# Raw keys per batch, node masks loaded once, and stores that alternate with fetches on the GpSimd queue of a two-layer graph kernel

## The chip, the core and the metric

The kernel runs on one NeuronCore of one Trainium2 chip. The core has five instruction queues: TensorE (PE), VectorE (DVE), ScalarE (ACT), GpSimd (POOL) and SyncE (SP, which only issues DMAs). The metric is the device time of one execution in microseconds (us). A change of under about 1% (19 us) can't be told from no change here: three runs of this same kernel lie between 1901.12 and 1918.54 us.

## The reference, cut to what matters

Sixteen graphs ("batches") of 1024 nodes with 64 channels go through two layers. In the first, every node receives the adjacency-weighted mean of its neighbours. In the second, each node drops some of its neighbours ("dilation"), takes three quantiles of each channel over the neighbours that are left, and runs a small two-layer perceptron on the result.

```
# layer 0
h = max(layernorm(x), 0)
x = x + (adj / clip(sum(adj, 2), 1)) @ h
# layer 1
h = max(layernorm(x), 0)
adj_ = where(eye, 1, adj);  nb = (adj_ > 0) & ~eye;  m = nb.sum(-1)
rank = cumsum(nb, -1) - 1
skip = where(m > 10, (m + 1) // 2, 1);  do_dil = (skip > 1) & mask
removed = nb & do_dil & ((rank + 1) % skip == 0)
valid = where(removed | removed.T, 0, adj_) > 0
agg = sum over tau of weight * (quantile tau of h over the valid neighbours)
y = (relu((h + agg) @ W1 + b1) @ W2 + b2) * mask
x = x + y
```

`adj` is 16 x 1024 x 1024 in float32 (64 MB). Most of it is zero: a node has a list of neighbours, short for most nodes and long for a few. `nodemask` is 16 x 1024 bytes.

## The kernel before, in words

**Lists instead of matrices.** The kernel turns each row of `adj` into a list of neighbour numbers, sorts all nodes of a group of four batches by the length of their lists, and then works on 128 nodes at a time whose lists have nearly the same length. It runs in two parts that overlap:

- *Per batch* (loops over 16 batches, each with eight blocks of 128 rows). `loads` (line 570) fetches `xt` (the nodes), `mrow` (the mask, 8 x 128 bytes) and eight tiles `at` of `adj`, all on SP. `beginnings` (588) normalises the nodes on ACT and DVE, and turns the mask on PE so that nodes lie on partitions. `signs` (610) takes signs on ACT; `listing` (627) multiplies them with a descending key (`keyed`) and takes the eight largest keys of each quarter row, 32 in all, into `rec`. `transposes` and `products` (667 on) do layer 0 on PE. `channels` (733) normalises again, into `row`. `endings` (747) writes the 32 keys of each node into `row` beside its channels, works out the node's place in the sorted order, and scatters the eight blocks of `row` to `srt` in DRAM with eight indirect DMAs on POOL.
- *Per group* of four batches. `group` (1196) reads the sorted keys back as `recs`, merges them to at most 16 per node (`keys`), and makes indices of them (`idx`). Then it adds one `Job` (841) for each list length. A job fetches neighbours' rows with one indirect DMA on POOL for every 128 neighbours (`places<-tab`), removes the dropped ones, sorts on DVE with a network of min and max, weighs, sums on PE, runs the perceptron, and stores 128 finished rows with one indirect DMA on POOL (`out_dram<-y`). Four lists of the longest nodes go through `long_lists` (1333) at the end (`lplaces<-whole`).

**What sets the order.** The order of DVE and POOL is written out by a planner (`Plan`, line 236) while the program is built, and the other queues are ordered from it. Streams of work yield the engine that they need next, the time from which they are ready, and a rank; `run` always takes the stream with the smallest pair (time at which it can begin, rank), so the rank decides only among streams that can begin at once. In this order each engine then works strictly in sequence. `endings` asks for POOL with a rank of `rank - 3000`, ahead of everything. Fetches of short jobs have the rank 100 times their group's number, plus a small number; stores of finished rows take the rank -1000 while fewer than 16 fetches of begun jobs are still to be issued, and 5000 otherwise (`urgent`). `scatter` (828) puts a one-column memset (`turn`) between two scatters to the same tensor that would follow each other directly. A buffer `places` is one of four, so that a fetch may have to wait until an earlier job is done with its buffer.

**What the change and the prediction touch.**

- Keys. `keyed` counts down over a whole row from a start that depends on the block of 128 rows, so `rec` holds N + 128 t - j for neighbour j of a node in block t. In `endings` eight ACT instructions, one per block, subtract 128 t and clip at zero while they copy to `row` (`bias=before[:, t:t + 1]`, lines 757 to 760).
- Masks. Sixteen small DMAs (576), casts (593), PE transposes (604) and ACT copies (606, 607: mask and node number into the last two columns of `row`).
- Stores. The rank function `first` (749) of the scatter of `row`, and the POOL request of `layers` (1190) for finished rows.

Of the kernel before, what the change touches and what calls it, by code (L numbers as in the profile page):

```python
# [9 lines left out]
F32 = mybir.dt.float32  # L10
# [233 lines left out]
class Plan:  # L244
# [25 lines left out]
    def room(self, name, bufs):  # L270

        tiles = self.slots.get(name, ())
        if len(tiles) < bufs:
            return 0.0
        old = tiles[-bufs]
        return INF if self.users[old] else max(self.used.get(old, 0.0), self.ready.get(old, 0.0))

    def at(self, *tiles):
        return max(self.ready.get(t.tensor.name, INF) for t in tiles)
# [104 lines left out]
def list_path(ctx, tc, x, adj, nodemask, w1, b1, w2, b2, out, go):  # L384
# [93 lines left out]
    wt0 = consts.tile([P, 1], F32, name="wt0")  # L478
    nc.vector.memset(wt0, QUANTILES[0][1])

    before = consts.tile([P, NT], F32, name="before")
    nc.vector.tensor_scalar(before, col_f[:, :NT], -float(P), None, op0=OP.mult)

    idle = consts.tile([P, 1], F32, name="idle")
    turn = consts.tile([P, 1], F32, name="turn")
# [80 lines left out]
    def known(st, *names):  # L566

        return max(at(st[name]) if name in st else INF for name in names)

    def loads(pool, now):  # L570
        def nodes(st, b):
            yield "SP", lambda: room("xt", 3)
            st["xt"] = new(pool, [P, NT, C], F32, "xt", 3, users=1)
            nc.sync.dma_start(st["xt"], x[b].rearrange("(t p) c -> p t c", p=P))
            st["mrow"] = new(tiny, [NT, P], U8, "mrow", 3)
            nc.sync.dma_start(st["mrow"], nodemask[b].rearrange("(t p) -> t p", p=P))

        yield from nodes(batch[0], 0)
        for b, st in enumerate(batch):
            now[0] = b  # L580
            for t in range(NT):
                if t == 2 and b + 1 < B:
                    yield from nodes(batch[b + 1], b + 1)
                yield "SP", lambda: room("at", 5)
                st["rows"][t] = new(pool, [P, N], F32, "at", 5, users=2)
                nc.sync.dma_start(st["rows"][t], adj[b, t * P:(t + 1) * P, :])

    def beginnings(pool, now):

        for b, st in enumerate(batch):  # L590
            now[0] = b
            yield "DVE", lambda: max(known(st, "xt", "mrow"), room("h0", 3), room("row", 4))
            mrow_f = new(tiny, [NT, P], F32, "mrow_f", 2)
            nc.vector.tensor_copy(mrow_f, st["mrow"])

            h0 = new(pool, [P, NT, C + 1], F32, "h0", 3, users=2)
            nc.vector.memset(h0[:, :, C:], 1.0)
            row = st["row"] = new(pool, [P, NT, RW], F32, "row", 4, users=1)
            nc.vector.memset(row[:, :, C:W], -1.0)
            yield from normed(h0[:, :, :C], st["xt"])  # L600
            st["h0"] = h0
            yield "PE", lambda: max(at(mrow_f), room("ps_small", 3))
            pm = new(ps_s, [P, HALF], F32, "ps_small", 3, users=1)
            nc.tensor.transpose(pm[:, :NT], mrow_f, ident[:NT, :NT])
            yield "ACT", lambda: at(pm)
            nc.scalar.copy(row[:, :, RW - 1], pm[:, :NT])
            nc.scalar.copy(row[:, :, RW - 2], row_f)
            free(pm)

    def signs(pool, now):  # L610
        for b, st in enumerate(batch):
# [134 lines left out]

    def endings(pool, now):

        first = lambda rank: rank - 3000
        for b, st in enumerate(batch):  # L750
            now[0] = b
            g = max(g for g in range(NG) if FIRST[g] <= b)
            size = GROUPS[g]
            yield "ACT", lambda: known(st, "rec", "row") if st["listed"] == NT else INF
            rec, total, row = st["rec"], st["total"], st["row"]

            for t in range(NT):
                nc.scalar.activation(
                    row[:, t, R0:R0 + 8 * NSEG], rec[:, t, :], AF.Relu, bias=before[:, t:t + 1]
                )  # L760


            yield "DVE", always
            found = new(pool, [P, NT, 8 * NSEG], BF, "found", 1)
            nc.vector.tensor_scalar(found, rec, 0.0, None, op0=OP.is_gt)
            d = new(tiny, [P, NT], F32, "d", 2)
            nc.vector.tensor_reduce(d, found, AX.X, OP.add)
            full = new(tiny, [P, NT], F32, "full", 2)
            nc.vector.tensor_reduce(
                full, found.rearrange("p t (s e) -> p t s e", e=8)[:, :, :, 7], AX.X, OP.max  # L770
            )
            nc.vector.scalar_tensor_tensor(d, full, float(STEPS[0]), d, op0=OP.mult, op1=OP.max)
            nc.vector.tensor_scalar(d, d, float(STEPS[0]), None, op0=OP.min)
            for s in STEPS[1:]:
                nc.vector.scalar_tensor_tensor(d, total, float(s), d, op0=OP.is_gt, op1=OP.add)
            free(rec)
            free(total)
            hot = new(tiny, [P, CLS, NT], BF, "hot", 2)
            nc.vector.tensor_tensor(
                hot, cls, d.unsqueeze(1).to_broadcast([P, CLS, NT]), OP.is_equal  # L780
            )
            yield "PE", lambda: max(at(hot), room("ps_small", 3))
            pc = new(ps_s, [P, HALF], F32, "ps_small", 3, users=1)
            K = CLS * NT
            flat = hot.rearrange("p c t -> p (c t)")
            nc.tensor.matmul(pc[:, :K], earlier, flat, start=True, stop=True)
            nc.tensor.matmul(pc[:, K:2 * K], ones, flat, start=True, stop=True)
            yield "DVE", lambda: at(pc) + SLACK
            base = new(tiny, [P, K], F32, "base", 2)
            nc.vector.tensor_tensor_scan(  # L790
                base, pc[:, K:2 * K], zeros[:, :K], 0.0, op0=OP.add, op1=OP.add
            )
            nc.vector.tensor_tensor(base, base, pc[:, K:2 * K], OP.subtract)
            nc.vector.tensor_tensor(base, base, pc[:, :K], OP.add)
            free(pc)
            nc.vector.tensor_tensor(base, base, flat, OP.mult)
            pos = new(tiny, [P, NT], F32, "pos", 2)
            nc.vector.tensor_reduce(pos, base.rearrange("p (c t) -> p t c", t=NT), AX.X, OP.add)
            low = new(tiny, [P, NT], I32, "low", 2)
            nc.vector.tensor_copy(low, pos)  # L800
            nc.vector.tensor_scalar(low, low, LSUB - 1, None, op0=OP.bitwise_and)
            if size == 2:
                aside = new(tiny, [P, 2, NT], F32, "aside", 2)
                for e, by in enumerate((-32.0, 64.0)):
                    nc.vector.tensor_scalar(
                        aside[:, e, :], pos, 64.0 / (e + 1), by, op0=OP.is_lt, op1=OP.mult
                    )
                for e in range(2):
                    nc.vector.tensor_tensor(pos, pos, aside[:, e, :], OP.add)
            nc.vector.tensor_scalar(  # L810
                pos, pos, float(size), float(LSUB * (b - FIRST[g])), op0=OP.mult, op1=OP.add
            )
            to = new(pool, [P, NT], I32, "to", 2)
            nc.vector.scalar_tensor_tensor(to, low, float(1 - size), pos, op0=OP.mult, op1=OP.add)
            for t in range(NT):
                yield "POOL", lambda: max(at(to), at(row)) + LOOSE if "normed" in st else INF, first
                scatter(srt[g], row[:, t, :], to[:, t:t + 1], sorts[g])
            free(row)
            progress["batches"] = b + 1
# [21 lines left out]
    class Job:  # L841
# [291 lines left out]
        def layers(self, terms, sources):  # L1133
# [53 lines left out]
                free(py)  # L1187

            for t in range(T):
                yield "POOL", lambda: at(y) + LATE  # L1190
                top = HP if self.half and t == 0 else P
                scatter(out_rows, y[:top, t, :], self.nodes_i[:top, t:t + 1], scatters)
            free(y)
# [2 lines left out]
    def group(g, kept=grp, name=""):  # L1196
# [53 lines left out]
        keys = new(kept, [P, NTAU, 16], F32, name + "keys", 1 if name else 2)  # L1250
        nc.vector.memset(keys, 0.0)
        left = tiny.tile([P, 8 * NSEG], F32, name="left")
        for t in range(begin, NTAU):
            nc.vector.max(out=keys[:, t, :8], in_=lists[:, t, :])
            if caps[t] > 8:
                nc.vector.match_replace(
                    out=left, in_to_replace=keys[:, t, :8], in_values=lists[:, t, :],
                    imm_value=0.0,
                )
                nc.vector.max(out=keys[:, t, 8:], in_=left)  # L1260
            if t % 8 == 0:
                yield "DVE", always

        assert all(cap <= T_THRESH for cap in caps[begin + 1:])
        fst = slice(begin, begin + 1)
        skip = dilation(m[:, fst], mask[:, fst], 1)
# [462 lines left out]
```

## Time and profile before

| | |
|---|---|
| median of three runs | 1902.93 us (1901.12, 1902.93, 1918.54) |
| the profiled execution, whole | 1904.97 us |
| its span, first to last instruction | 1902.9 us, 16005 instructions |
| indirect DMAs on POOL | 931: 128 of `srt<-row`, 496 of `places<-tab`, 163 of `lplaces<-whole`, 128 of `out_dram`, 8 of `tab<-drop`, 8 of `gat_rows` |
| start of the eight scatters of a batch | 68, 101, 140, 176 us for the first four, then 243, 284, 376, 492, 585, 642, 738, 826, 949, 981, 1098, 1139 us |
| start of the last group's fetch of `gat_rows` | 1161 us |
| memsets `turn` | 215, 25.7 us busy |

All times below come from that one execution, which is 2.04 us longer than the median. A row of the profile names engine, operation, the tile written and the tiles read, the number of instructions, their summed and mean time, and the time in which the engine stood idle ahead of them together with what ended it. "issue" there means that the engine waited for nothing that the profile shows, "remote" that the releaser is not known. Since nearly all instructions are recorded under the one line of the planner's wrapper (L238), groups are told apart by their tiles.

### The profile page before, as it was taken

How to read it: one execution, taken by the hardware profiler on the slowest of the kernel's cores; microseconds unless marked ns; L12 is line 12 of the kernel's file. 1: busy time of each engine (PE TensorE's matmuls, PEld its weight loads, DVE VectorE, ACT ScalarE, POOL GpSimd, SP SyncE). 2: the span in 40 equal slices, each digit the busy share in tenths (PEclk: the TensorE clock that was granted, in tenths of full speed). 3: DMA queues.
4: the chain of work that ended last, by engine and by line, in shares of the span. 5: the costliest groups of instructions: out<-in, count | busy, mean ns of one | idle time of the engine just before them, and what ended most of it. 6: DMA issues, size and time to landing. Idle time of an engine off the chain costs nothing. (4 is left out here: it accounts for less than half of the span.)

```text
span 1902.9 us, 16005 instructions
## 1 busy us (share of the span) xinstructions
PE 807.9 (42%) x3192; PEld 505.9 (27%) x3192; DVE 1203.3 (63%) x4137; ACT 825.4 (43%) x2773; POOL 944.8 (50%) x1155
## 2 busy tenths in 40 slices
PE   5787742263681565447355822002200000443456
PEld 3333321232340343234133321001100000343334
DVE  7866944874672577365627746795227859796552
ACT  7987844554680556363665520012101114613142
POOL 0123255463557436543764455667772750446653
PEclk8887865576775776668676765555555555675566
DMA  5536633232442233333242123211110110101210
GB/s 163 164 116 164 195 101 90 63 75 54 104 145 52 71 116 80 87 73 112 65 125 52 24 52 80 49 38 38 27 27 9 25 19 0 19 17 31 41 25 15
DMA packets 135718, 133.36 MB, mean 70 GB/s; under 512 B 100756, under 2 KB 103444, under 8 KB 135492
## 3 DMA queue, kind: packets, MB, share of 16 engines
q1 hardware_dynamic: 102876, 90.79, 17.1%
q0 software_dynamic: 32736, 41.47, 10.1%
q14 instruction: 78, 0.64, 0.1%
q8 instruction: 28, 0.46, 0.1%
HBM read 112.90 MB, written 23.61 MB: 72 GB/s over the span
## 5 line engine op out<-in xcount | busy, mean ns | idle before, releaser
L238 POOL DMA_INDIRECT places<-tab,idx x372 | 360.9, 970 | 220.1 <-issue 106.6
L238 PE MATMUL pt<-ident,prod 128*128 128x128 f32 (+1 forms) x736 | 172.6, 397 | 550.8 <-ACT prod L238 231.8
L238 PE MATMUL pt<-ident,at 128*128 128x128 f32 x1024 | 195.4, 343 | 240.9 <-ACT att L238 102.7
L238 PEld LDWEIGHTS pt<-ident,prod 128*128 128x128 f32 (+1 forms) x736 | 138.5, 273 | 588.3 <-ACT prod L238 386.0
L238 PE MATMUL ps_small<-att,h 128*65 128x512 f32 x512 | 267.4, 670 | 28.0 <-ACT att L238 9.3
L238 POOL DMA_INDIRECT srt<-row,to x128 | 126.1, 985 | 235.0 <-ACT row L238 193.5
L238 PEld LDWEIGHTS pt<-ident,at 128*128 128x128 f32 x1024 | 150.3, 177 | 292.9 <-ACT att L238 123.0
L238 ACT COPY att<-pt 128x512 f32<-128x512 f32 x256 | 143.5, 582 | 153.8 <-remote 94.7
L238 POOL DMA_INDIRECT places<-tab,last_idx x124 | 124.8, 1006 | 147.0 <-ACT prod L238 79.8
L238 DVE MAX8 rec<-sg 128x8 f16<-128x256 f16 x512 | 180.2, 414 | 13.0 <-remote 7.2
L238 POOL DMA_INDIRECT lplaces<-whole,lidx x163 | 162.5, 997 | 49.7 <-issue 49.1
L238 POOL DMA_INDIRECT out_dram<-y,nodes_i x93 | 93.1, 1002 | 123.1 <-DVE y L238 79.5
L238 ACT ACTIVATE sg<-at 128x1024 f16<-128x1024 f32 x128 | 134.7, 1053 | 36.9 <-DMA at<-in_adj_dram 27.6
L238 ACT COPY ot<-pt 128x128 f32<-128x128 f32 (+3 forms) x56 | 21.9, 395 | 256.5 <-remote 132.8
L238 ACT ACTIVATE places<-places,gone 128x64 f32<-128x64 f32 x466 | 117.4, 335 | 16.6 <-issue 6.1
L238 PEld LDWEIGHTS ps_small<-att,h 128*65 128x65 f32 x512 | 78.1, 158 | 170.1 <-issue 137.0
L238 ACT ACTIVATE prod<-places,w 128x64 f32<-128x64 f32 x227 | 60.3, 337 | 115.4 <-DVE w L238 80.3
L238 PE MATMUL ps_small<-ot,w_sb 128*128 128x128 f32 (+3 forms) x112 | 52.9, 568 | 127.2 <-issue 61.5
L238 DVE TENSOR_TENSOR sg<-sg,keyed 128x1024 f16<-128x1024 f16 x128 | 87.4, 683 | 21.0 <-ACT sg L238 19.7
L238 DVE TENSOR_TENSOR other<-places,other 128x64 f32<-128x64 f32 (+6 forms) x204 | 69.7, 342 | 30.0 <-issue 7.8
L238 DVE TENSOR_TENSOR places<-places,other 128x64 f32<-128x64 f32 (+2 forms) x208 | 62.4, 309 | 29.2 <-DVE other L238 12.1
L238 DVE TENSOR_TENSOR places<-other,places 128x128 f32<-128x128 f32 (+5 forms) x160 | 55.1, 345 | 21.8 <-DVE other L238 5.9
(256 smaller groups left out, 1715.5 us busy)
## 6 DMA issues: line engine op xcount, KB each, us to landing
at<-in_adj_dram SPq DMA_DIRECT2D x128, 512.0 KB
places<-tab,idx POOLq DMA_INDIRECT x372
whole<-tab SPq DMA_DIRECT2D x4, 1057.0 KB
tab<-row SPq DMA_DIRECT2D x16, 264.0 KB
xt<-in_x_dram SPq DMA_DIRECT2D x16, 256.0 KB
lplaces<-whole,lidx POOLq DMA_INDIRECT x163
srt<-row,to POOLq DMA_INDIRECT x128
places<-tab,last_idx POOLq DMA_INDIRECT x124
```

What stands on the lines that cost most here:

```text
L238: ins = getattr(self._engine, op)(*args, **kwargs)
```

## The change

1. *Keys.* `endings` copies all 32 x 8 keys of a batch as they are, with one ACT copy in place of eight biased Relus. `group` works out the first node number of each sorted node's block (`ahead`, from the node number with its low seven bits cleared), subtracts it from the merged keys, and clips at zero. These are five more DVE instructions per group: two casts and a shift over 128 x 32, a subtraction and a clip over 128 x 512.
2. *Masks.* One DMA of 128 x 128 bytes, one DVE cast, one PE transpose and two DVE copies at the start make a table `marks` of mask and node number for all batches. Per batch one ACT copy of 128 x 8 x 2 takes the place of the DMA, the cast, the transpose and two ACT copies.
3. *Stores.* After one scatter of `row`, the next has the rank 50 instead of `rank - 3000`. After one store of finished rows, the next has the rank 20000. Both hold only while no other POOL instruction has come since.

```diff
-    before = consts.tile([P, NT], F32, name="before")
-    nc.vector.tensor_scalar(before, col_f[:, :NT], -float(P), None, op0=OP.mult)
+    mrow = consts.tile([B * NT, P], U8, name="mrow")
+    nc.sync.dma_start(mrow, nodemask.rearrange("b (t p) -> (b t) p", p=P))
+    mrow_f = grp.tile([P, N], F32, name="gat_rows", bufs=1)[:B * NT, :P]
+    nc.vector.tensor_copy(mrow_f, mrow)
+    pm = ps_s.tile([P, HALF], F32, name="ps_small")
+    nc.tensor.transpose(pm[:, :B * NT], mrow_f, ident[:B * NT, :B * NT])
+    marks = consts.tile([P, B, NT, 2], HF, name="marks")
+    nc.vector.tensor_copy(
+        marks[:, :, :, 1].rearrange("p b t -> p (b t)"), pm[:, :B * NT]
+    )
+    nc.vector.tensor_copy(
+        marks[:, :, :, 0], row_f.unsqueeze(1).to_broadcast([P, B, NT])
+    )
...
-            st["mrow"] = new(tiny, [NT, P], U8, "mrow", 3)
-            nc.sync.dma_start(st["mrow"], nodemask[b].rearrange("(t p) -> t p", p=P))
...
-            mrow_f = new(tiny, [NT, P], F32, "mrow_f", 2)
-            nc.vector.tensor_copy(mrow_f, st["mrow"])
...
-            yield "PE", lambda: max(at(mrow_f), room("ps_small", 3))
-            pm = new(ps_s, [P, HALF], F32, "ps_small", 3, users=1)
-            nc.tensor.transpose(pm[:, :NT], mrow_f, ident[:NT, :NT])
-            yield "ACT", lambda: at(pm)
-            nc.scalar.copy(row[:, :, RW - 1], pm[:, :NT])
-            nc.scalar.copy(row[:, :, RW - 2], row_f)
-            free(pm)
+            yield "ACT", lambda: at(row)
+            nc.scalar.copy(row[:, :, RW - 2:], marks[:, b, :, :])
...
-        first = lambda rank: rank - 3000
+        first = lambda rank: 50 if plan.last is sorts[g] else rank - 3000
...
-            for t in range(NT):
-                nc.scalar.activation(
-                    row[:, t, R0:R0 + 8 * NSEG], rec[:, t, :], AF.Relu, bias=before[:, t:t + 1]
-                )
+            nc.scalar.copy(row[:, :, R0:R0 + 8 * NSEG], rec)
...
-                yield "POOL", lambda: at(y) + LATE
+                yield "POOL", lambda: at(y) + LATE, lambda rank: (
+                    20000 if plan.last is scatters else rank
+                )
...
+        low = new(grp, [P, NTAU], I32, "own_tile", 1)
+        nc.vector.tensor_copy(low, node)
+        nc.vector.tensor_scalar(
+            low, low, 7, 7, op0=OP.logical_shift_right, op1=OP.logical_shift_left
+        )
+        ahead = new(grp, [P, NTAU], F32, "own_first", 1)
+        nc.vector.tensor_copy(ahead, low)
...
+        nc.vector.tensor_tensor(
+            keys, keys, ahead.unsqueeze(2).to_broadcast([P, NTAU, 16]), OP.subtract
+        )
+        nc.vector.tensor_scalar(keys, keys, 0.0, None, op0=OP.max)
```

More of the change, by code (lines that the diff above doesn't have):

```diff
@@ L591, in beginnings @@
             now[0] = b
-            yield "DVE", lambda: max(known(st, "xt", "mrow"), room("h0", 3), room("row", 4))
-            mrow_f = new(tiny, [NT, P], F32, "mrow_f", 2)
-            nc.vector.tensor_copy(mrow_f, st["mrow"])
+            yield "DVE", lambda: max(known(st, "xt"), room("h0", 3), room("row", 4))
             h0 = new(pool, [P, NT, C + 1], F32, "h0", 3, users=2)
```

## The prediction

> **What bounds the kernel now.** I read the page first, for a full engine:
>
> ```profile
> span 1902.9 us, 16005 instructions
> PE 807.9 (42%) x3192; PEld 505.9 (27%) x3192; DVE 1203.3 (63%) x4137; ACT 825.4 (43%) x2773; POOL 944.8 (50%) x1155
> ```
>
> There is none: the busiest, DVE, works 63% of the span. The chain of waits breaks off at 1781 us, so it says nothing of the rest. So I went to the waits of POOL, which fetches and stores everything:
>
> ```profile
> POOL srt L238 <- ACT row L238: 193.5, 25, 64.4
> POOL places L238 <- issue: 172.3, 466, 24.0
> POOL out_dram L238 <- DVE y L238: 116.1, 12, 28.8
> ```
>
> (us in total, times, longest.) Of the 193.5 us, 142 lie before 176 us, while the first four batches have nothing else for POOL. Hardly any instruction waits for a job's fetch to land: among the sixteen longest waits of DVE, ACT and PE, before and after 1150 us, one such line stands, 2.2 us of PE. POOL's timeline gives the pace of its two kinds of work:
>
> ```profile
> 584.86 1.00 POOL L238 DMA_INDIRECT srt<-row,to  x1 [0.30 <-issue]
> 585.86 0.12 POOL L238 MEMSET turn<- 128x1 f32 x1
> 586.16 0.99 POOL L238 DMA_INDIRECT srt<-row,to  x1 [0.18 <-issue]
> ...
> 598.86 0.94 POOL L238 DMA_INDIRECT places<-tab,idx  x1 [0.30 <-issue]
> 600.11 0.94 POOL L238 DMA_INDIRECT places<-tab,idx  x1 [0.30 <-issue]
> ```
>
> A scatter with its memset takes 1.27 to 1.30 us from start to start, a fetch 1.25 us. The last view is the busy time of the engines in stretches (PE, weight loads, DVE, ACT, POOL, then clock, DMA share, GB/s):
>
> ```profile
> 410.00:420.00 10.00, 8.95 (x33) 5.36 (x33) 8.37 (x33) 8.56 (x27) 6.70 (x7) 0.69 0.36 93
> 420.00:430.00 10.00, 5.79 (x25) 2.78 (x23) 2.85 (x12) 2.54 (x15) 7.56 (x9) 1.00 0.17 29
> 430.00:440.00 10.00, 0.00 (x0) 0.00 (x0) 0.00 (x0) 0.00 (x0) 7.56 (x9) 0.50 0.18 27
> 440.00:450.00 10.00, 0.69 (x4) 0.51 (x4) 0.00 (x0) 1.14 (x3) 3.99 (x5) 0.50 0.10 17
> 450.00:460.00 10.00, 4.26 (x18) 3.39 (x19) 5.22 (x12) 9.38 (x35) 0.00 (x0) 0.50 0.33 80
> ```
>
> Here 27 POOL DMAs follow each other without a pause, and everything else comes to a halt until some 6 us after the last. This repeats. I cut POOL's timeline into runs (starts under 2.2 us apart) and looked up how busy PE, DVE and ACT together were in the 2.5 us stretch of each DMA: 4.99 of 7.5 us for the first eight of a run (364 DMAs), 3.43 for the 9th to 16th (236), 1.37 from the 17th on (331: 124 between 226 and 1161 us, 207 after). So the bound is an alternation: POOL works in long runs while the others stand, then they work while POOL waits for a row, a result or a buffer. A DMA beyond the 16th costs the others 1.26 x (1 - 1.37 / 4.99) = 0.91 us, about 300 us in all. Whether the run causes the halt, or both come from one wait, the trace doesn't tell.
>
> **What the Trainium skill says.** "ScalarE: Activation LUTs", section *What ACT_TABLE_LOAD costs*: an activation with a bias pointer takes about 280 + 0.833 N ns, one without 186 + 0.833 N, neighbours overlap by 93 ns. For N = 32 that is 307 ns; the trace has 317 for the eight Relus, and five of them in 1.16 us, so it agrees. "SBUF — State Buffer", *Who interferes with whom*, says that only VectorE and GpSimd can block each other, and that "PE and ACT never wait on anyone". It doesn't explain the halts above, in which ACT and PE stop too.
>
> **The change part by part.**
>
> *Keys, ACT.* Eight Relus at 0.22 us pitch (0.317 less the overlap) take 1.8 us per batch. The one copy of 256 columns is not in the trace: the nearest row, `ot<-pt` of 128x256 from PSUM, has 0.364 us, the skill's formula gives 0.40. Relief: 1.8 - 0.4 = 1.4 us per batch, and about 0.1 for two small copies (0.173 and 0.206 us) becoming one: 1.5 x 16 = 24 us of ACT. What of it counts? In the first 200 us ACT is busy 86% and 80%, POOL waits for ACT's `row`, and nothing hides it: 4 x 1.5 = 6 us. For the other twelve batches, 18 us, ACT is about half busy, and the tile view of the Relus shows that hardly anybody waits right behind them (6.5 us PE's weight loads, 0.4 us POOL). Bounds 0 and 18; I take half, 9.
>
> *Keys, DVE.* Per group: cast 0.2, shift 0.19 and cast 0.2 over 128 x 32 (casts of 8 columns take 0.17), a subtraction over 128 x 512 at 0.69 (the row of `lplaces<-l0other`, 128x512), a clip at 0.36 (half of the 0.694 us of a comparison over 1024 columns): 1.64 us. They stand between `recs` and `idx`, behind them DVE's dropping step, then POOL's scatter `tab<-drop` and every fetch of the group. Four groups: 0 to 6.6 us, taken in full, since POOL stands at the beginning of the first and the last group (17.3 us for `tab`, 16.9 for `gat_rows`).
>
> *Masks.* Gone: 16 DMAs (SP, 0.306 us each, 4.9 in all), 16 casts (DVE, 0.207: 3.3), 16 transposes (PE, 0.224: 3.6). SP waits for PE anyway (342.8 us, 93 times), and nobody waits for the cast or the transpose by the tile view, so 0 for these; the cover is gone only where SP would run ahead of PE. Added at the start, a wait: DVE now stands until the mask is in and PE has turned it, and the order of the new program puts that transpose behind PE's first sixteen of `at`, which end at 14.8 us in the trace. Behind it in DVE's queue are `none`, `keyed` and the first `ln_s` and `sg`, which began at 12.1 us and would begin near 17.5. For `none` wait SP's four `tab<-none` and the sixth load of `at` behind them. DVE has 23% idle in the first 100 us to catch up: 0 to 6 us, I take 3.
>
> *Stores.* In the new order POOL has 106 memsets instead of 215. At 1.27 against 1.25 us of pace that is worth 109 x 0.02 = 2 us at most, as the gap after a DMA shrinks by what the memset takes. The scatters of batches 4 to 7 alternate with fetches one by one; from batch 8 on they alternate only with stores, or go in blocks as before; finished rows alternate with fetches throughout. A block of eight scatters holds the fetches behind it up for 10.2 us, one of twelve stores for 15; alternating halves that for the fetch in the middle. But total work on POOL stays 931 DMAs. What is moved past: the scatters end up to 10 us later, and the group reads `recs` only after the last of them. The order of POOL shows it as a wash: the first DMA of groups 1, 2 and 3 has place 202, 379 and 544 before, and 210, 363 and 549 now. Bounds: nothing where no fetch is waited for (the waits above speak for that), 5 us for each of the four scatter blocks and four longest store blocks, 40 us. I take 20.
>
> *Sum* against the profiled 1904.97: -6 - 9 + 6.6 + 3 - 20 = -25, so 1880; against the median 1902.93, 1878. I say **1879 us**.
>
> **Rivals.**
>
> *Hidden.* The profile shows no one waiting for fetches to land, and ACT's relief beyond the first four batches has work beside it. Then only -6 + 6.6 + 3 = +4 stays: 1907, between 1890 and 1921. For it: the missing waits, and the nearly equal places in POOL's order. Against: queues are strictly ordered, so a shorter ACT block moves all behind it.
>
> *Longer runs (slower).* Fetches and stores that alternate fill the places where POOL now pauses for a scatter's row or a result: between 240 and 1150 us it waits 17 times for `row` (51.1 us) and 3 times for `y` (48.7 us). Each pause that goes joins two runs and puts the second's DMAs beyond the 16th place, at 0.91 us each to the others. It decides once more than 28 DMAs are moved there in sum (28 x 0.91 = 25 us eats the gain). If four runs of 16, the mean between 226 and 1161 us, are joined to long ones, that is 64 DMAs or 58 us: 1879 + 58 = 1937, between 1922 and 1970. For it: 21 runs are longer than 16 already. Against: the dependences that make POOL pause are still there.
>
> *Shorter runs.* The same price with the other sign, where alternation spreads the waits for `y` over the runs: 40 DMAs fewer, 1843.
>
> *It doesn't do what it says.* True in part: rows alternate with fetches for four batches only. It is inside the cases above.
>
> **How the numbers follow.** A difference under 1% (19 us) can't be told from none. The sum 0.37 (1855 to 1903, two thirds of it faster by over 1%, under 1884), hidden 0.25, longer runs 0.26, shorter runs 0.12. Faster 0.25 + 0.12 + 0.03 for a hidden case that comes out low = 0.40; slower 0.26 + 0.01 = 0.27; the rest, 0.33, within 1%. Range 1838 to 1948: it takes in the shorter runs' value and most of the longer runs'; the likeliest case alone has 1855 to 1903.
>
> **What would show it.** Relief: ACT's busy time down by some 35 us (the removed instructions' own time: 36.1 + 6 less 9), and the scatters of the fourth batch beginning near 170 us instead of 176. Start: the first `sg` product on DVE near 17 us. Groups: `tab<-drop` 1.6 us later after `recs`. Stores: the start of the last group's `gat_rows` under 1161 us by the 15 to 20 us of the sum. Runs: the number of POOL DMAs from the 17th place on against 331; if it rises by 30 or more and the time falls nonetheless, my reading of the halts is wrong. If the span before 226 us is shorter and the rest longer by more than that, the longer-run rival holds. The prediction fails if the time is over 1922 or under 1838.

## The result and the profile after

The changed kernel takes **1929.65 us** (median of four runs, 1919.67 to 1937.27), the one before 1902.03 beside it: ratio 1.011, 95% interval 1.006 to 1.016. It is slower by some 28 us; forecast were 1879 us and a gain. The page of the changed kernel's profile:

```profile
span 1930.9 us, 15718 instructions
PE 810.8 (42%) x3177; PEld 497.7 (26%) x3177; DVE 1203.2 (62%) x4138; ACT 810.4 (42%) x2676; POOL 934.3 (48%) x1046
```

287 instructions fewer, ACT 15 us less busy, DVE the same, and a span 28 us longer: every engine waits more. POOL's waits:

```profile
POOL srt L238 <- ACT row L238: 205.3, 16, 65.3
POOL places L238 <- ACT prod L238: 172.3, 7, 57.7
POOL places L238 <- issue: 143.9, 472, 0.3
POOL out_dram L238 <- DVE y L238: 88.0, 8, 22.2
POOL out_dram L238 <- DVE ln_v L238: 42.4, 1, 42.4
```

The waits for `row` fell from 25 to 16 but take no less time (193.5 us before). The two ahead of stores make 130 us (125 before), and the wait for `prod` to be done with a `places` buffer grew from 110.1 us in five to 172.3 in seven. The lines of before that the prediction does not show:

```profile
POOL places L238 <- ACT prod L238: 110.1, 5, 72.8
POOL out_dram L238 <- DVE ln_v L238: 8.9, 1, 8.9
```

POOL's timeline after the change shows the new alternation:

```profile
604.63 1.00 POOL L238 DMA_INDIRECT out_dram<-y,nodes_i  x1 [0.30 <-issue]
605.94 0.98 POOL L238 DMA_INDIRECT srt<-row,to  x1 [0.31 <-DMA places<-tab,idx]
607.23 0.96 POOL L238 DMA_INDIRECT out_dram<-y,nodes_i  x1 [0.30 <-issue]
608.49 0.96 POOL L238 DMA_INDIRECT srt<-row,to  x1 [0.30 <-issue]
```

The pace is what it was, 1.26 to 1.31 us from start to start; that half of the memsets are gone (106 of 215 are left) buys nothing. The busy times in stretches (columns as in the prediction) show the longest halt:

```profile
620.00:630.00 10.00, 0.54 (x2) 0.36 (x2) 1.41 (x4) 0.00 (x0) 7.56 (x9) 0.50 0.18 37
630.00:640.00 10.00, 0.00 (x0) 0.00 (x0) 0.00 (x0) 0.00 (x0) 7.56 (x9) 0.50 0.16 27
640.00:650.00 10.00, 0.00 (x0) 0.00 (x0) 0.00 (x0) 0.00 (x0) 7.56 (x9) 0.50 0.17 27
...
660.00:670.00 10.00, 6.35 (x24) 4.36 (x24) 4.84 (x15) 8.24 (x25) 0.00 (x0) 0.61 0.30 79
```

POOL issues 61 DMAs from 575 to 651 us without a pause, the others hardly work from 600 to 650, and then POOL stands until 710. Cut into runs as in the prediction, 379 DMAs lie from the 17th place on, against 331 before. So far it looks like the rival *Longer runs*: 48 x 0.91 = 44 us. By stages: the last group's fetch of `gat_rows` begins at 1205 us in place of 1161, 44 us late, and the rest is 16 us shorter (726 for 742).

**Two kinds of chip.** The experiments fell on several chips. On three of them the kernel before takes 1478 to 1482 us, and nothing halts; on two it takes 1908 and 1944 us with the halts of the first profile. No chip was met at two times, so these runs don't tell whether the halts belong to the chip or to the time; "a chip with halts" leaves that open. All ratios below are to the kernel before on the same chip.

### The profile page after: what moved, and what is told of

It reads as the page before. It is cut to its first block, busy times and chain, and to the rows that moved or that the text cites. A ratio compares the mean times of both kernels' runs of the same rounds, so it can differ in the third digit from the quotient of the medians.

```text
span 1930.9 us, 15718 instructions
## 1 busy us (share of the span) xinstructions
PE 810.8 (42%) x3177; PEld 497.7 (26%) x3177; DVE 1203.2 (62%) x4138; ACT 810.4 (42%) x2676; POOL 934.3 (48%) x1046
## 5 line engine op out<-in xcount | busy, mean ns | idle before, releaser
L238 PE MATMUL ps_small<-att,h 128*65 128x512 f32 x512 | 271.8, 683 | 57.3 <-issue 36.4
L238 ACT ACTIVATE places<-places,gone 128x64 f32<-128x64 f32 x496 | 124.9, 335 | 7.7 <-issue 6.1
L238 DVE TENSOR_TENSOR other<-places 128x128 f32<-128x128 f32 (+3 forms) x80 | 28.5, 357 | 71.2 <-remote 33.2
```

The source lines that it names most:

```text
L238: ins = getattr(self._engine, op)(*args, **kwargs)
```

## The experiments

**The parts alone.** `km` is the changed kernel with the ranks of the stores as before (parts 1 and 2), `stores` the kernel before with the two rank functions of part 3, `keys` and `masks` are parts 1 and 2 singly. `b2` and `a2` are the two kernels unchanged.

```diff
 km
-        first = lambda rank: 50 if plan.last is sorts[g] else rank - 3000
+        first = lambda rank: rank - 3000
...
-                yield "POOL", lambda: at(y) + LATE, lambda rank: (
-                    20000 if plan.last is scatters else rank
-                )
+                yield "POOL", lambda: at(y) + LATE
```

Expected of `km`:

> The change without part 3 (keys and masks only, the ranks of the stores as before). Theory R (long unbroken runs of indirect DMAs on POOL stop the other engines, and part 3 made them longer): the terms for keys and masks alone remain, -6 - 9 + 6.6 + 3 = -5 us, so about 1897 us (1885 to 1910), and the number of POOL DMAs from the 17th place of a run on stays near 331 (310 to 350). Rival K (the keys' five DVE instructions per group and the wait for the mask at the start are what costs): 1915 to 1935 us.

Of `stores`:

> The kernel before with part 3 alone (both ranks). Theory R: slower by 25 to 45 us, so 1927 to 1947 us, with 370 or more POOL DMAs from the 17th place of a run on, against 331. Rival K (keys and masks cost): 1880 to 1905 us, and no more DMAs in long runs.

Of `b2`, `a2`, `keys` and `masks`, which ran after these two:

> The kernel before, unchanged, to have its own trace beside the others. Theory E (the halts of all engines, some 420 us of the first profile, belong to the chip or the execution on which it was taken, not to the program): about 1482 us, no halts, over 600 POOL DMAs from the 17th place of a run on with some 4.4 of 7.5 us busy beside them. Theory P (they belong to the program and come and go): between 1480 and 1900 us, with halts in part of the executions.

> The changed kernel, unchanged, beside the one before on one chip. If the parts add up (keys and masks +53 us, stores +10 us in the runs so far): ratio near 1.04. If the first comparison holds whatever the chip does: 1.006 to 1.016. If the loss came from the halts alone, as theory R had it: 0.98 to 1.00 where there are no halts.

> The kernel before with part 1 alone (keys copied raw, shifted per group). Keys and masks together were 53 us slower than before. Theory W (the work itself: five DVE instructions per group stand before everything that POOL fetches): at most 4 x 1.7 = 7 us slower, ratio 1.000 to 1.005. Theory L (a new order of the planner leaves one long gap late in POOL's queue): the ratio can be 1.02 to 1.04 in either part, with one gap of over 30 us in POOL after 1150 us.

> The kernel before with part 2 alone (masks loaded and turned once). Theory W: 0 to 6 us slower by the wait at the start, ratio 1.000 to 1.004, and the first scatter of rows some 3 us later (71 us for 68). Theory L: 1.02 to 1.04 if the gap of over 30 us in POOL after 1150 us stands in this run's trace, and about 1.00 to 1.01 if not.

| kernel | ratio to before, 95% interval | us (before beside it) | POOL pauses over 5 us after 1150 us |
|---|---|---|---|
| stores | 1.0075 (1.0047 to 1.0102) | 1491.6 (1481.7) | 19 |
| km | 1.0349 (1.0301 to 1.0397) | 1534.9 (1481.7) | 44, 7 |
| keys | 0.9910 (0.9882 to 0.9939) | 1468.2 (1479.3) | 6 |
| masks | 1.0295 (1.0251 to 1.0338) | 1523.2 (1479.3) | 28, 26, 7 |
| a2, the whole change | 1.0209 (1.0176 to 1.0242) | 1511.0 (1479.3) | 6 |
| b2, the kernel before | 1.0017 (1.0000 to 1.0033) | 1481.5 (1479.3) | 7 |

All on chips without halts. Three things follow. The change is slower there too, by 31 us, so it needs no halts for that. By stages it is even the same shift: the last `gat_rows` at 952 us for 903, 49 us late, the rest 17 us shorter. And the parts don't add up: by their ratios masks alone cost 44 us, keys alone gain 13, both together cost 52, and all three only 31. No count of instructions does that. In `km` and `masks`, which lose most, the loss lies behind the last `gat_rows` (619 and 624 us from there to the end, for 574 in `b2`), where POOL has one or two long pauses (the last column); theory L had put those down to the planner's order. The forecasts mostly missed: `stores` and `a2` fell between their ranges, `km` above both of its ranges and `keys` below both. `masks` fits L's range, with two pauses of 28 and 26 us in place of one over 30, and `b2` is as theory E had it.

**Work and order apart.** Two pairs of kernels make a square. In `masks_f` and `km_f` the new instructions are issued, but the planner is told the old ones (`ghost`), so that POOL's order is that of the kernel before exactly, and DVE's too but for what is removed or added. In `masks_o` and `after_o` the old instructions are issued while the planner is told the new ones. "Order" means the planner's whole plan here: it also decides whether ACT or DVE does a job's subtractions and products, and so the plan of the changed kernel has 496 subtractions on ACT and that of before 466, whichever work is issued.

```diff
 masks_f and km_f
+    raw = nc
     nc = plan.nc
+    ghost = lambda engine, op, *args: plan.note(engine, op, args, {})
...
-            nc.vector.tensor_copy(mrow_f, st["mrow"])
+            ghost("DVE", "tensor_copy", mrow_f, st["mrow"])
...
-            nc.scalar.copy(row[:, :, RW - 1], pm[:, :NT])
-            nc.scalar.copy(row[:, :, RW - 2], row_f)
+            ghost("ACT", "copy", row[:, :, RW - 1], pm[:, :NT])
+            ghost("ACT", "copy", row[:, :, RW - 2], row_f)
+            raw.scalar.copy(row[:, :, RW - 2:], marks[:, b, :, :])
```

> Parts 1 and 2 (keys and masks) at work, but the planner is told the old instructions, so that POOL's order is that of the kernel before exactly and DVE's too, but for the instructions that parts 1 and 2 remove and add. Keys and masks with their own order were at 1.035. Theory L (what costs is the new order that the planner makes of the changed costs): 0.985 to 1.000, the work itself being worth -5 us or a little better (keys alone 0.991). Theory W (the work itself costs): 1.02 to 1.035 again.

> The other half of the square: the old work (eight Relus per batch, masks per batch) in the order that the changed kernel has on POOL and DVE, the ranks of the stores included. Theory L: as slow as the changed kernel or slower, 1.015 to 1.035. Theory W: 0.995 to 1.010, since the work is that of before.

> Part 2 (masks) at work with the order of the kernel before on POOL and DVE. With its own order it was at 1.0295 with two gaps of 28 and 26 us in POOL after 1290 us. Theory L: 0.995 to 1.005, without those gaps. Theory W: 1.02 to 1.03.

> The work of the kernel before in the order that part 2 has. Theory L: 1.02 to 1.035, with gaps of over 20 us in POOL between 1280 and 1360 us. Theory W: 0.995 to 1.005.

| | order of before | own order |
|---|---|---|
| work of before | 1 | after_o 1.0139 (1.0088 to 1.0191); masks_o 1.0328 (1.0272 to 1.0384) |
| new work | km_f 0.9999 (0.9961 to 1.0037); masks_f 0.9968 (0.9939 to 0.9996) | the first result: 1.011 (1.006 to 1.016); masks, on a chip without halts: 1.0295 (1.0251 to 1.0338) |

The four new kernels ran on one chip with halts, so they bear on the first result. There the order costs and the work doesn't, as theory L had it. Two details are not as forecast: `after_o` lies just under L's range, which began at 1.015, and `masks_o` has no pause of over 20 us between 1280 and 1360 us; its long ones lie between 1480 and 1816 us. `km_f` and `after_o`, profiled on the same chip, show the known shift again: last `gat_rows` at 1172 and 1215 us (43 late), and 770 and 744 us from there to the end. The number of DMAs from the 17th place on doesn't tell which order is slow: `after_o` has 379 as the changed kernel, `km_f` 332, and `masks_o`, the slowest of all, 310.

`km_f` was repeated:

> Parts 1 and 2 at work in the order of the kernel before, with six buffers y as before. With seven it was at 1.0099 where the kernel before takes 1478 us, without, at 0.9999 where that takes 1944. If this chip is of the first kind: 0.993 to 1.003 if the seventh buffer (which lets SP fetch y earlier, ahead of loads of at) is what cost, and 1.007 to 1.013 if the work of parts 1 and 2 costs there, where POOL and DVE are fuller. If it is of the second kind: 1.000 again.

It met another chip with halts: 0.9982 (0.9949 to 1.0015). So on two such chips the work of parts 1 and 2 costs nothing that can be seen. On a chip without halts this pair was not run; `km_f_seven` below is the nearest to it.

**Any new order.** If the order is what costs, then an edit that does nothing but draw it anew must move the time too.

```diff
 slack
-SLACK = 2.0
+SLACK = 2.1
```

> The kernel before with one constant of the planner changed (SLACK 2.0 to 2.1 us): no instruction is added, removed or altered, only the order is drawn anew. Theory L (any new order may cost or gain one to three per cent, whatever the edit that caused it): away from 1.000 by more than 0.007, in either direction. Theory S (the orders that the planner finds are alike, and the parts of the change make theirs worse): 0.995 to 1.005.

Measured: **1.0294** (1.0256 to 1.0333), 1523.2 us for 1478.4, with no other line of the source changed (the plan that came of it has 20 more subtractions and 20 fewer products on ACT than that of before). POOL's waits from 1150 us on show where, `slack` first, then the kernel before (`b2`):

```profile
POOL places L238 <- ACT wu L238: 48.0, 2, 47.7
```

```profile
POOL places L238 <- ACT prod L238: 7.0, 1, 7.0
```

In the 47.7 us POOL waits for one `places` buffer. DVE isn't idle then:

```profile
1313.00:1363.00 50.00, 12.95 (x65) 11.42 (x66) 46.95 (x197) 8.43 (x35) 1.99 (x3) 0.57 0.02 5
```

DVE (the third of the busy times) works 46.95 of the 50 us, ACT and PE 8 and 13. What it does is sorting: of long lists (`lother`, `lplaces`) among the jobs whose buffers POOL needs, and so it does in the pauses of `masks`. That this sequence of DVE makes the pause is read from the trace, not tried.

**Through which wait.** In `a2` no late pause stands out, and the loss lies ahead of the last `gat_rows`. DVE's waits between 214 and 950 us, `b2` first, then `a2`:

```profile
DVE rem L238 <- DMA places<-tab,idx: 20.7, 8, 4.9
...
DVE sg L238 <- ACT sg L238: 12.9, 3, 8.7
...
DVE ln_v L238 <- ACT ln_sq L238: 5.6, 3, 3.4
```

```profile
DVE sg L238 <- ACT sg L238: 46.2, 6, 15.7
DVE rem L238 <- DMA places<-tab,idx: 24.0, 5, 11.1
...
DVE ln_v L238 <- ACT ln_sq L238: 14.2, 5, 6.7
DVE rem L238 <- DMA srt<-row,to: 6.3, 1, 6.3
```

DVE waits 33 us longer for signs from ACT, and 9 for its squares. The longest of these waits, followed back through the timelines of DVE, ACT and SP:

```profile
524.15 0.69 DVE L238 TENSOR_TENSOR sg<-sg,keyed 128x1024 f16<-128x1024 f16 x1 [15.74 <-ACT sg L238]
```

```profile
522.97 1.06 ACT L238 ACTIVATE sg<-at 128x1024 f16<-128x1024 f32 x1 [18.44 <-DMA at<-in_adj_dram]
```

```profile
495.77 0.38 SPq L238 DMA_DIRECT2D tab<-row  x1
518.25 0.36 SPq L238 DMA_DIRECT2D y<-srt  x1
518.70 0.45 SPq L238 DMA_DIRECT2D at<-in_adj_dram  x1
```

```profile
SPq L238 <- DMA out_dram<-y,nodes_i: 21.9, 1, 21.9
```

SP stands 21.9 us because the store of finished rows that frees a `y` hasn't landed; the load of `at` is queued behind, and ACT, PE and DVE all stand. In sum such waits are not peculiar to the slower order, `b2` first, then `a2`, between 214 and 950 us:

```profile
SPq L238 <- DMA out_dram<-y,nodes_i: 207.9, 26, 30.0
```

```profile
SPq L238 <- DMA out_dram<-y,nodes_i: 220.6, 28, 24.8
```

To try this path, I gave `y` a seventh buffer, in the changed kernel (`after_seven`) and in `km_f` as its control (`km_f_seven`):

```diff
-            y = new(mlp, [P, T, CO], F32, "y", 6, users=1)
+            y = new(mlp, [P, T, CO], F32, "y", 7, users=1)
```

> The changed kernel with seven buffers y in place of six; its order on POOL and DVE is exactly that of the changed kernel, and only SP may fetch the next y one store earlier. In the changed kernel's trace of 1508.8 us SP stood 21.9 us (496 to 518 us) before a fetch of y because the store of an older y had not landed, the loads of at behind it came late, and ACT, PE and DVE all stood for 15 to 18 us. Theory Y (the stores that were put behind fetches hold the y buffers, and SP's strict order turns that into late loads for everybody): the ratio to the kernel before falls from 1.011 to 1.021 to about 1.000 to 1.010, some 10 to 25 us less than the changed kernel. Theory D (the loss is spread over many small waits of the new order): at most 5 us less, 1.010 to 1.020.

> Parts 1 and 2 at work in the order of the kernel before (0.9999 of it in the run so far), with seven buffers y. It is the control for the run above and a candidate for the best version. Theory Y: the kernel before has the same kind of wait (255 us of SP in 27 waits between 200 and 1250 us), so it gains too: 0.985 to 0.995. Theory D: 0.995 to 1.003.

Measured 1.0208 (1.0181 to 1.0235) and 1.0099 (1.0076 to 1.0122), on a chip without halts. Neither gained; 1.0208 is just above theory D's range, and 1.0099 above both ranges of the control. But the first says less than it was meant to, for its trace still has the wait:

```profile
SPq L238 <- DMA out_dram<-y,nodes_i: 22.0, 1, 22.0
```

SP had taken up one more `y` by then and met the same late store. The wait wasn't removed, so how much of the 31 us passes through it stays open. Why `km_f_seven` is slower there stays open too, since `km_f` with six buffers has met only chips with halts. The buffer need not be the reason: before the first `y` is fetched, at 191.9 us, DVE has stood 9.0 us until PE had turned the masks, and the fourth batch's scatters begin at 173.8 us, for 165.8 in `b2` and 170.5 in `d40_again` below, which has the old work on the same chip. So without halts the work may cost some microseconds after all, up to the 1% of this run.

**Do long runs of POOL DMAs halt the others?** The trace of before couldn't tell. Forty fetches that nobody needs were put at the head of POOL's queue, where it is idle until 68 us. The order of all other instructions stays word for word the same.

```diff
 d40
     plan = Plan(nc)
+    for k in range(40):
+        if k % 16 == 0:
+            junk = gat.tile([P, 16, 1, W], F32, name="places", bufs=4)
+        nc.gpsimd.indirect_dma_start(
+            out=junk[:, k % 16, 0, :C], out_offset=None, in_=x.rearrange("b n c -> (b n) c"),
+            in_offset=bass.IndirectOffsetOnAxis(ap=row_i[:, :1], axis=0),
+        )
```

> The kernel before with 40 more indirect fetches (128 rows of 256 bytes each) in a row at the head of POOL's queue, into memory that nobody reads; the order of the instructions on PE, DVE, ACT and SP is unchanged. They fill some 50 us from about 4 to 54 us, where POOL is idle until 68 us, and nobody waits for them. Theory R (the run itself stops the others from about the 17th DMA on): PE, DVE and ACT come to a halt between about 25 and 55 us (under 1.5 of 7.5 us busy in a stretch of 2.5 us), 24 DMAs at 0.91 to 1.25 us give 22 to 30 us more: 1924 to 1932 us. Rival O (the halts are waits for results that POOL brings, and the run only goes with them): no halt, 1897 to 1908 us.

> The same 40 fetches in five runs of eight, with POOL busy for some 7 us with sixteen iotas (128x256) after each but the last; POOL is done near 84 us, so its first scatters begin some 16 us late, which the first group need not feel. Theory R: no run reaches the 17th place, so no halt, within 8 us of the kernel before (1895 to 1910 us). If a pause of this kind does not release the others, it is as slow as the 40 in a row: 1924 to 1932. Rival O: 1897 to 1912 us too, so this run tells only together with the 40 in a row.

> Again the kernel before with 40 fetches in a row at the head of POOL's queue, order otherwise unchanged. On a chip where the kernel before takes about 1480 us it was at 0.998 and showed no halt. If this chip is one where it takes 1900 us or more: theory R (the run itself halts the others there) 1.010 to 1.016, with PE, DVE and ACT under 1.5 of 7.5 us busy between about 25 and 55 us; theory O (halts come only where the others wait for POOL's results) 0.997 to 1.003, no halt there.

> Once more the 40 fetches in a row at the head of POOL's queue. If this chip is one where the kernel before takes 1900 us or more: theory R (a long run itself halts the others there) 1.010 to 1.016, with PE, DVE and ACT under 1.5 of 7.5 us busy between about 25 and 55 us; theory O (halts come only where the others wait for POOL's results) 0.997 to 1.003 and no halt there. If it is one of about 1480 us, 1.000 as twice before, and the question stays open.

`d40`, `d40p` and `d40_again` met chips without halts: 0.9984 (0.9968 to 1.0000), 0.9988 (0.9967 to 1.0008) and 1.0006 (0.9992 to 1.0021). Nothing halts in them, so the pauses of `d40p` told nothing. `d40_third` met a chip with halts (before: 1907.8 us). Busy times from 25 us on, first `d40_again`, then `d40_third`, the same program:

```profile
25.00:30.00 5.00, 5.00 (x12) 1.72 (x12) 3.81 (x12) 5.00 (x17) 3.78 (x5) 0.75 0.68 186
...
40.00:45.00 5.00, 5.00 (x18) 3.24 (x17) 4.66 (x18) 4.52 (x11) 3.78 (x4) 0.54 0.60 163
45.00:50.00 5.00, 5.00 (x13) 1.64 (x12) 4.90 (x12) 4.21 (x13) 3.96 (x4) 1.00 0.29 102
50.00:55.00 5.00, 4.71 (x34) 3.29 (x33) 4.83 (x14) 3.84 (x10) 3.78 (x5) 1.00 0.53 141
```

```profile
25.00:30.00 5.00, 0.71 (x4) 0.31 (x2) 1.51 (x5) 0.00 (x0) 3.78 (x5) 0.50 0.09 26
...
40.00:45.00 5.00, 0.72 (x4) 0.72 (x5) 0.00 (x0) 1.25 (x3) 3.78 (x5) 0.62 0.10 28
45.00:50.00 5.00, 5.00 (x10) 1.53 (x8) 0.00 (x0) 0.00 (x0) 3.78 (x5) 0.70 0.09 26
50.00:55.00 5.00, 0.20 (x1) 0.00 (x0) 0.00 (x0) 0.86 (x3) 3.78 (x5) 0.99 0.10 26
```

POOL does the same in both. PE, DVE and ACT together work 92 of 3 x 35 us between 20 and 55 us in one, and 28.5 in the other. They wait for nothing that POOL brings. What a halt looks like from within, in `d40_third`:

```profile
24.59 1.11 PE L238 MATMUL pt<-ident,at 128*128 128x128 f32 x4 [3.14 <-issue]
32.44 0.58 ACT L238 COPY att<-pt 128x512 f32<-128x512 f32 x1 [7.90 <-remote]
33.08 1.11 PE L238 MATMUL pt<-ident,at 128*128 128x128 f32 x4 [7.37 <-issue]
```

The copy reads what PE has turned. PE's last work before it ends at 25.70 and ACT does nothing in between, yet the copy begins at 32.44. So it isn't the work waited for that came late; what released the copy is not known ("remote"). Between 20 and 100 us ACT stands 30.2 us ahead of four such copies, and 0.6 us in `d40_again`.

The first scatters begin at 100 us in place of 68 in the first profile. So on such a chip a long run does halt the others: theory R, with 32 us for the 24 of the forty DMAs beyond the 16th, 1.3 us each on the spot. Its details are less exact: between 25 and 55 us the three engines work 1.7 of 7.5 us, forecast were under 1.5. And the trace cuts the forty into a run of 4 and one of 36, and the others stand from about 25 us, when the second is at its 13th. The end is later by less, 1.0076 (1.0043 to 1.0110), 14.5 us or 0.6 each, under the 1.010 to 1.016 that R expected: already the last `gat_rows` is only 17 us late (1178 for 1161), as later pauses take up the rest.

## Why the prediction was wrong

*The failed step* is the **Stores** term of the sum, -20 us, and with it the way in which the sum prices things. Every edit is priced by the instructions that it adds, removes or moves, each against the order of before, and the new order counts as "a wash" by the places of three DMAs in POOL's queue (202, 379, 544 against 210, 363, 549). No term stands for the order being drawn anew on DVE and POOL, though every changed cost does that. Where -20 us were forecast, the runs show +11 us for the ranks alone (`stores`, 1.0075 on a chip without halts) and +1.4% or 27 us for the whole new order under the old work (`after_o`). How much of the 27 us is the alternation that part 3 wanted, and how much came with the redrawing, isn't told apart: no kernel with part 3 alone, and none with parts 1 and 2 in their own order, met a chip with halts.

- *Keys and masks as work*: the sum was -6 - 9 + 6.6 + 3 = -5.4 us. `km_f` gives -0.2 us (-8 to +7) and -3.4 (-10 to +3). On chips with halts the size is borne out within that; *Hidden*'s +4 lies inside it too, so the 9 us for later batches are neither shown nor excluded. The five DVE instructions of a group were priced rightly: 7.0 us for all four groups, forecast 6.6.
- *ACT's busy time*, forecast down by 35 us, fell by 15. The rows themselves were right: on the chip without halts the eight Relus and two copies of a batch took 36.2 + 3.2 + 2.8 = 42.2 us over all batches, the copies in their place 6.5 + 3.1 = 9.6. But neighbours overlap, so the engine gains less than the rows: under the old order (`km_f`) it fell by 24.2 us, the 24 that the prediction itself had from the pitch. The new order took off another part, for it gave ACT 30 more subtractions (`places<-places,gone` 496 for 466, +7.8 us), which DVE had done in two instructions.
- *The fourth batch's scatters* were to begin near 170 us in place of 176. They begin at 178. With the old work in the same order it is 185 (`after_o`), with the new work in the old order 174 and 175 (`km_f`, `km_f_again`): a relief of 1 to 7 us, and a new order that costs more.
- *The start*: DVE's first `sg` product begins at 16.5 us, near the 17 forecast. The wait is there, but costs nothing that remains: `masks_f`, which has it, is at 0.997.
- *Stores*: the last `gat_rows` came 44 us later, not 15 to 20 earlier. The memsets fell from 215 to 106 for no gain, as bounded (2 us).
- *Longer runs*, the rival that ended slower, named 1922 to 1970 us, and the time fell there. Its signs came true: DMAs from the 17th place on rose by 48, and the first group's `gat_rows` began 4 us earlier (200.6 for 204.4 us) while the rest took 32 us longer. Its mechanism is real (`d40_third`), and at the 0.6 us of that run 48 DMAs would be 29 us, all of the loss. Still it can't be what decides everywhere: without any halts the changed kernel loses as much (31 us), and the order with fewest such DMAs is slowest (`masks_o`). What part of the 28 us the halts make up on the first chip stays open.
- *"Hardly any instruction waits for a job's fetch to land"* was read from a trace with halts, which holds fewer than half of the events (last section), so that many waits in it are put down to "remote" or "issue". In `b2`, the same program with the events there, DVE waits 50 us for fetches in 14 waits, of which the longest kind is this:

```profile
DVE rem L238 <- DMA places<-tab,last_idx: 26.6, 5, 17.9
```

- *Shorter runs*: didn't happen.

## What to carry to other kernels

Where a planner writes the order from modelled costs, any edit that touches a modelled cost can draw a new order, and here that alone moved the time by up to 3.3% (`masks_o`): a tenth of a microsecond in one constant cost 2.9%. So judge the work with the order frozen (tell the planner the old instructions) and on both kinds of chip, judge orders separately, and believe no saving that is smaller than the spread of the orders. The keys alone in their own order are the one version faster than both kernels (0.991, on a chip without halts), and that too may be the order's doing.

## What the hardware showed beyond expectation

The same program takes 1478 to 1482 us on three chips and 1908 to 1944 on two. DVE's busy time is nearly equal (1203.3 us in the first profile, 1200.1 in `b2`); its whole difference is waiting. Without halts the kernel before has 641 POOL DMAs from the 17th place of a run on, beside 4.30 of 7.5 us of work on the others; with halts 331, beside 1.37. Why POOL's run stops the others on some chips isn't known. One trait goes with it: the eight traces with halts hold 10,056 to 10,657 semaphore events each, the twelve without 24,980 to 26,053 (counted from the traces). Whether the missing events are a part of the cause or of the recording wasn't tried. Every execution here has a recorded span and clock beside its time, so it is open too whether the halts would be there without any recording.
